# State products of an attention and MLP layer in four row groups and four PSUM banks, with the first transfers in another order

## The chip, the cores and the metric

The kernel runs on one core of a Trainium2 chip. Its engines work side by side, each through its own queue in order: TensorE (PE, with its weight loads PEld), VectorE (DVE), ScalarE (ACT), GpSimd (POOL) and SyncE (SP), which here issues the transfers. The metric is device time in microseconds (us). A page and a trace come from one execution that the hardware profiler recorded; its span runs from the first to the last instruction.

## The reference, cut to what matters

A layer for 8 sequences of 256 tokens of width 256: layer norm, then an attention with 16 heads and an MLP, both from the same normed input, added to the residual. All is float32. Per head, with 64 states:

```python
q, k = rope(hs @ Wq.T), rope(hs @ Wk.T)            # 128 a head
s = clip(hs @ Ws1.T @ Ws2.T + bs2, -32, 32)         # rank 16, then 64 states a head
z = cumlogsumexp(s, axis=tokens); es = exp(s); enz = exp(-z)
A = tril(q @ k.T * scale)
ok = enz * (A @ es)
W2 = tril((softmax(ok) * enz) @ es.T)
o = W2 @ v
o = o * rsqrt(mean(o * o) + eps) * g_norm_weight * silu(hs @ Wg.T)
out = o @ Wo.T
```

The MLP (2048 wide) has weights that come as 4-bit codes with scales, and are decoded on the chip.

## The kernel before

The 2048 tokens are taken in four groups of 512 (two sequences each), and the 16 heads in eight pairs: 32 steps of one group and one head pair, group after group. The main loop runs n from -1 to 32. In an iteration it prepares step n + 1 (`states` and the four `rope` calls, which make q and k), computes the scores of step n (`scores`, `logits`, `softmax`, and `value` and `gate`), and finishes step n - 1 (`turn`, `cross`, `weights`, `apply`, `outputs`, `turn_back`; every second time `close`, the output projection). Pieces of the MLP (`ffn`) and of the decoding (`decode_next`) are strewn between, so that TensorE has work while the attention's chain passes through the other engines.

The order is written by hand. Each piece has a place between 0 and 1 in the iteration: `POS` for all iterations, `START` for the first two, `NORM_AT` for the norm of a later token group, which `NORMS` puts into iterations 0, 2 and 5. `DUE` says how many decode pieces are to be issued by each iteration. The loop sorts the pieces by place and issues them. A piece issues its matmuls at once and leaves the work of the other engines as a generator in `chains`; after each piece `tick()` moves each generator on by one stage. So the places also decide how the queues of VectorE, ScalarE and GpSimd are ordered.

PSUM has eight banks of 512 float32 a partition. `bank()` gives one; where it is still read, the first matmul that writes it waits. The norm's scaled half and the rope's scratch share two buffers under one name, `z`.

`low_rank` (L374) makes the rank-16 product for a token group: two matmuls with `w_s1`, then one ScalarE copy with a bias, `one_at`, that sets row 16 of every group of 32 rows to one, so that the bias `bs2`, which lies as row 16 below `Ws2` in `w_s2`, is added by the second product. `rT` and `w_s2` hold two copies, at rows 0 and 32. `states` (L391) needs the second product both ways round: tokens by states (`es`, L402, from rows 0 to 16) and states by tokens (`esT`, L403, from rows 32 to 48). Each is four matmuls of 17 rows by 128 columns into one bank. VectorE clamps both (L413), ScalarE takes the exponential (L416), VectorE sums along the tokens (L421) and takes reciprocals (L427).

`rope` (L432): two matmuls (L438), two ScalarE copies that swap halves (L447, L448), one VectorE product with cos (L449), two GpSimd operations (L451, L452). `norm` (L185): VectorE statistics (L192 to L194), a GpSimd power (L195), the scaling into `z` (L198), transposes on TensorE (L206), a ScalarE copy to `xT` (L212). `softmax` begins with transposes (L548). `weights` multiplies (L618), and VectorE masks the two banks (L626).

Of the kernel before, what the change touches and what calls it, by code (L numbers as in the profile page):

```python
# [10 lines left out]
F32 = mybir.dt.float32  # L11
I32 = mybir.dt.int32
AF = mybir.ActivationFunctionType
ALU = mybir.AluOpType
# [18 lines left out]
POS = {'scores': (0.059, 0.112),  # L33
 'turn': (0,),
 'logits': (0.144,),
 'softmax': (0.255,),
 'cross': (0.143,),
 'weights': (0.179, 0.209),
 'low': (0.176,),
 'states': (0.223,),  # L40
 'outputs': (0.364, 0.394),
 'back': (0.647, 0.702),
 'close': (0.136, 0.286),
 'rope': (0.36, 0.45, 0.54, 0.63),
 'vg': (0.45, 0.55, 0.75, 0.88)}
START = {-1: {'states': (0.534,), 'rope': (0.3, 0.4, 0.5, 0.6)},
 0: {'vg': (0.0, 0.03, 0.06, 0.229),
     'scores': (0.2, 0.28),
     'states': (0.342,),
     'logits': (0.34,),  # L50
     'softmax': (0.5,),
     'rope': (0.16, 0.24, 0.32, 0.45)}}
FEED = {-1: (0.452, 1.0)}
NORMS = {0: 1, 2: 2, 5: 3}
NORM_AT = (0.2, 0.293, 0.427, 0.639, 0.75, 0.938)
FIRST = [0.35, 1.41]
LAST = [2.16, 2.05]
DUE = [4, 6, 6, 7, 8, 8, 10, 10, 11, 12, 12, 13, 14, 15, 15, 16, 17, 18, 18, 19, 20, 22, 23, 23, 24]


@with_exitstack
def layer_kernel(ctx: ExitStack, tc: tile.TileContext, a: dict, out: bass.AP):
# [74 lines left out]
    w_s1 = const.tile([P, 2, 64], F32, tag="w_s1", name="w_s1")  # L137
    w_s2 = const.tile([64, H * M], F32, tag="w_s2", name="w_s2")
    one_at = const.tile([64, 1], F32, tag="one_at", name="one_at")
# [17 lines left out]
    def load_w(n, k):  # L157

        if n < N:
            w = aw.tile([P, 2, 2, 2 * DK], F32, tag=f"wts{k}", name=f"wts{k}")  # L160
            nc.sync.dma_start(out=w, in_=a["wqkvg"][steps[n][1]][:, k : k + 2])
            wts[n, k] = w

    load_x(0, 2)
    load_x(2, 2)
    nc.sync.dma_start(out=w_s1.rearrange("p c f -> p (c f)"), in_=a["ws1"])
    nc.sync.dma_start(out=one_at, in_=a["one_at"])
    for r in (0, 32):
# [205 lines left out]
    def low_rank(g):  # L374

        need(*normed[g])
        rT = p1.tile([64, G], F32, tag="rT", name="rT")
        ps = bank()
        for c in range(2):
            nc.tensor.matmul(  # L380
                ps[0:64, :], lhsT=w_s1[:, c, :], rhs=xT[:, c, g * G : (g + 1) * G],
                start=c == 0, stop=c == 1,
            )

        def work():
            nc.scalar.activation(rT, ps[0:64, :], AF.Identity, bias=one_at)
            yield

        rTs[g] = rT, chain(work(), ps)

    def states(n):  # L391

        g, hp = steps[n]
        ms = slice(hp * P, (hp + 1) * P)
        (rT, c), to = rTs[g], of[n]
        need(c)
        es = to["es"] = new(p2, [P, TC, P], "es", 2)
        esT = to["esT"] = new(p2, [P, G], "esT", 2)
        ps, psT = bank(), bank()
        for i in range(TC):  # L400
            ts = slice(i * P, (i + 1) * P)
            nc.tensor.matmul(ps[:, ts], lhsT=rT[0:17, ts], rhs=w_s2[0:17, ms], start=True, stop=True)  # L402
            nc.tensor.matmul(  # L403
                psT[:, ts], lhsT=w_s2[32:49, ms], rhs=rT[32:49, ts], start=True, stop=True
            )


        enz = to["enz"] = new(p2, [P, G], "enz", 2)

        def work():  # L410
            both = ((esT, psT), (es.rearrange("p i m -> p (i m)"), ps))
            for t, q in both:
                nc.vector.tensor_scalar(t, q, CLAMP, -CLAMP, ALU.min, ALU.max)  # L413
            yield
            for t, q in both:
                nc.scalar.activation(t, t, AF.Exp)  # L416
            yield
            for b in range(2):
                e = esT[:, b * T : (b + 1) * T]

                nc.vector.tensor_tensor_scan(  # L421
                    enz[:, b * T : (b + 1) * T], e, e, 0.0, ALU.add, ALU.max
                )
            yield
            for i in range(TC):
                r = enz[:, i * P : (i + 1) * P]
                nc.vector.reciprocal(r, r)  # L427
                yield

        to["states"] = chain(work(), ps, psT, es, esT, enz)  # L430

    def rope(n, j, which):  # L432

# [373 lines left out]
def _layout(x):  # L807

    c = np.ascontiguousarray
    half = MLP // 2  # L810

    def pairs(ws):
        w = np.stack([w.T.reshape(P, 2, H // 2, 2 * DK) for w in ws])
        return c(w.transpose(3, 1, 0, 2, 4))

    def packed_in(w):
        return c(w.reshape(half, 2, -1).transpose(2, 1, 0).reshape(-1, MLP))

# [11 lines left out]
    return {  # L830
        "x": c(n[at + "hidden_states"].reshape(NTOK, D)),
        "wqkvg": pairs([n[at + w] for w in ("Wq", "Wk", "Wv", "Wg")]),
        "wo": c(n[at + "Wo"].T.reshape(H, DK, D).transpose(1, 0, 2)),
        "ws1": c(np.pad(n[at + "Ws1"].T.reshape(P, 2, 1, 16), [(0, 0)] * 3 + [(0, 16)]).repeat(2, 2).reshape(P, 128)),
        "one_at": (np.arange(64) % 32 == 16).astype(np.float32).reshape(64, 1),
        "ws2": c(n[at + "Ws2"].T),
        "bs2": c(n[at + "bs2"].reshape(1, H * M)),
        "gw": c(n[at + "g_norm_weight"].reshape(DK, 1)),
        "codes": quarters(lambda w: w, "_W_packed"),
        "scales": quarters(lambda w: w.repeat(16, 0), "_scales"),  # L840
        "cos": c(cos),
        "sin": c(sin),
    }
# [17 lines left out]
```

## Time and profile before

| | |
|---|---|
| time, median of 3 runs | 1268.24 us (1267.06 to 1269.0) |
| profiled execution, its own time | 1268.5 us |
| its span | 1266.5 us |
| busy DVE in the span | 795.7 us, 63% |
| first matmul | 7.08 us |
| end of the last matmul | 1262.3 us |
| all TensorE idle time up to the last matmul | 15.1 us |
| matmul records of L402 and L403 | 512, in 32 calls of 1.09 us |

The largest groups of TensorE are the products with the weights:

```profile
L438 PE MATMUL ps<-xT,wts 128*128 128x512 f32 x512 | 240.8, 593 | 0.0
L490 PE MATMUL ps<-wts,xT 128*128 128x256 f32 x1024 | 239.7, 379 | 0.0
```

A group line has the source line, engine and operation, what is written from what, the shapes and the count; then the busy time in us and the mean ns of one, then the idle time of the engine ahead of it. Matmuls overlap, so the mean of one is longer than the distance from one start to the next. A timeline line has start and length in us, engine, line and operation; in brackets is the engine's idle time ahead of it and what ended it. The list of waits has, for each pair, the us in all, the times and the longest.

### The profile page before, as it was taken

The numbers are of one execution on the slowest core, as the hardware profiler recorded it, in microseconds if no ns is written. First come the engines' busy times: TensorE is split into PE (matmuls) and PEld (weight loads), VectorE is DVE, ScalarE is ACT, GpSimd is POOL, SyncE is SP. The second block draws the span as 40 slices with busy tenths as digits, with TensorE's granted clock in tenths as the row PEclk, the third lists the DMA queues.
The fourth block names the chain that finished last, engine by engine and source line by source line (L and its number), as shares of the span: only waits on it lengthen the run. The fifth ranks groups of instructions, "written<-read, shape, count | busy, mean of one in ns | idle before, by whom it ended". The sixth has DMA issues, their size and how long they took to land.

```text
span 1266.5 us, 17998 instructions
## 1 busy us (share of the span) xinstructions
PE 1247.2 (98%) x6704; PEld 897.2 (71%) x6704; DVE 795.7 (63%) x1528; ACT 543.0 (43%) x1709; POOL 441.4 (35%) x408
## 2 busy tenths in 40 slices
PE   7999899999999999999999999999999999999998
PEld 4576676767777777767677686776777766777776
DVE  6967655766665666664765756666665566566443
ACT  2444335453444444452543534445443355445232
POOL 4444234441334443233443323444232444323311
PEclk9999999999999999999999999999999999999999
DMA  4301111011111100111110111101011110101000
GB/s 157 124 18 50 34 34 50 18 34 34 51 34 34 51 18 18 34 35 50 50 33 2 34 51 34 34 29 38 2 34 34 34 34 26 42 17 43 25 17 17
DMA packets 18362, 47.75 MB, mean 38 GB/s; under 512 B 1986, under 2 KB 6466, under 8 KB 18276
## 3 DMA queue, kind: packets, MB, share of 16 engines
q1 hardware_dynamic: 18276, 46.61, 11.5%
q8 instruction: 53, 0.87, 0.3%
q14 instruction: 33, 0.27, 0.1%
HBM read 44.51 MB, written 2.10 MB: 37 GB/s over the span
## 4 chain that ended last, share of the span: by engine, by line
PE 92%; DVE 5%; POOL 1%; issue 1%; ACT 1%; DMA 0%; POOLq 0%; DVEq 0%; ACTq 0%
PE ps L490 16%; PE ps L438 16%; PE ps L708 9%; PE ps L339 9%; PE ps L319 8%; PE ps L299 8%; PE ps L659 4%; PE ps L508 4%; PE ps L527 3%; PE ps L618 3%; PE ps L402 2%; PE ps L511 2%; PE ps L690 2%; PE ps L595 1%; PE ps L548 1%; PE ps L577 1%
## 5 line engine op out<-in xcount | busy, mean ns | idle before, releaser
L451 POOL TENSOR_TENSOR z<-z,sin 128x512 f32<-128x512 f32 x128 | 163.3, 1275 | 435.5 <-ACT z L448 434.8
L438 PE MATMUL ps<-xT,wts 128*128 128x512 f32 x512 | 240.8, 593 | 0.0
L490 PE MATMUL ps<-wts,xT 128*128 128x256 f32 x1024 | 239.7, 379 | 0.0
L490 PEld LDWEIGHTS ps<-wts,xT 128*128 128x128 f32 x1024 | 191.9, 190 | 55.8 <-issue 28.9
L438 PEld LDWEIGHTS ps<-xT,wts 128*128 128x128 f32 x512 | 94.3, 191 | 84.9 <-issue 77.8
L307 POOL TENSOR_SCALAR t<-t 128x512 f32<-128x512 f32 x64 | 40.2, 627 | 266.9 <-ACT t L305 256.5
L447 ACT COPY z<-ps 64x512 f32<-64x512 f32 x128 | 74.5, 582 | 129.8 <-PE ps L438 90.7
L299 PE MATMUL ps<-xT,w_gate 128*128 128x512 f32 x256 | 120.8, 594 | 0.0
L319 PE MATMUL ps<-xT,w_up 128*128 128x512 f32 x256 | 120.6, 593 | 0.0
L278 DVE TENSOR_TENSOR res<-ps,res 128x512 f32<-128x512 f32 x64 | 44.1, 689 | 117.0 <-PE ps L708 61.0
L427 DVE RECIPROCAL enz<-enz 128x128 f32<-128x128 f32 x128 | 116.7, 931 | 0.0
L339 PE MATMUL ps<-w_down,inter 128*128 128x256 f32 x512 | 116.0, 380 | 0.7 <-DVE inter L327 0.7
L708 PE MATMUL ps<-w_o,ogT 128*128 128x256 f32 x512 | 115.6, 379 | 0.0
L708 PEld LDWEIGHTS ps<-w_o,ogT 128*128 128x128 f32 x512 | 95.6, 190 | 14.6 <-issue 2.2
L339 PEld LDWEIGHTS ps<-w_down,inter 128*128 128x128 f32 x512 | 95.9, 190 | 14.2 <-DVE inter L327 1.5
L449 DVE TENSOR_TENSOR k<-ps,cos 128x512 f32<-128x512 f32 x64 | 43.9, 685 | 82.7 <-ACT z L448 82.7
L452 POOL TENSOR_TENSOR q<-q,z 128x512 f32<-128x512 f32 x64 | 81.6, 1274 | 21.6 <-DVE q L449 13.9
L452 POOL TENSOR_TENSOR k<-k,z 128x512 f32<-128x512 f32 x64 | 81.4, 1272 | 12.6 <-DVE k L449 8.3
L560 ACT ACTIVATE pr<-ps,mx 128x64 f32<-128x64 f32 x256 | 76.5, 325 | 12.8 <-DVE mx L557 12.8
L659 PEld LDWEIGHTS ps<-v,wt 128*128 128x128 f32 x512 | 65.0, 192 | 20.5 <-issue 19.8
L677 DVE SCALAR_TENSOR_TENSOR og<-ps,ss,sgate 128x128 f32<-128x128 f32 x256 | 70.0, 339 | 14.7 <-POOL ss L673 14.3
L673 POOL TENSOR_TENSOR ss<-ss,nhalf 128x4 f32<-128x4 f32 x64 | 64.8, 1017 | 39.8 <-DVE ss L672 38.1
(81 smaller groups left out, 1976.9 us busy)
## 6 DMA issues: line engine op xcount, KB each, us to landing
wts<-in_wqkvg_dram SPq DMA_DIRECT2D x64, 512.0 KB, 3.8
pk<-in_codes_dram SPq DMA_DIRECT2D x12, 256.0 KB, 4.7
sc<-in_scales_dram SPq DMA_DIRECT2D x12, 256.0 KB, 4.7
w_o<-in_wo_dram SPq DMA_DIRECT2D x4, 512.0 KB, 6.3
out_dram<-res SPq DMA_DIRECT2D x8, 256.0 KB, 2.1
res<-in_x_dram SPq DMA_DIRECT2D x3, 512.0 KB, 5.5
res<-in_x_dram SPq DMA_DIRECT2D x2, 256.0 KB, 3.4
w_s<-in_ws_dram SPq DMA_DIRECT2D x3, 64.0 KB, 2.8
```

The costliest lines, as they stand in the source:

```text
L299: nc.tensor.matmul(pg, lhsT=w_gate[:, c, ns], rhs=xT[:, c, gs], start=c == 0, stop=c == 1)
L319: nc.tensor.matmul(pu, lhsT=w_up[:, c, ns], rhs=xT[:, c, gs], start=c == 0, stop=c == 1)
L339: nc.tensor.matmul(ps[:, k, :], lhsT=inter[g, n][0][:, (i + k) * P : (i + k + 1) * P], rhs=w_dn[:, n, :], start=n == 2 * q, stop=n == 2 * ...
L427: nc.vector.reciprocal(r, r)
L438: nc.tensor.matmul(ps, lhsT=w[:, c, :], rhs=xT[:, c, g * G : (g + 1) * G], start=c == 0, stop=c == 1)
L447: nc.scalar.copy(z[0:64], pv[64:128])
L451: nc.gpsimd.tensor_tensor(z, z, sin_b, ALU.mult)
L452: nc.gpsimd.tensor_tensor(y, y, z, ALU.add)
L490: nc.tensor.matmul(ps[:, k, :], lhsT=xT[:, c, tt], rhs=w[:, which, c, :], start=c == 0, stop=c == 1,)
L560: nc.scalar.activation(pr[:, k, :], pv[:, k, :], AF.Exp, bias=mx[:, k : k + 1], scale=SCALE, accum_out=sm[:, k : k + 1],)
L659: nc.tensor.matmul(po[:, i, :], lhsT=wt[:, i, :], rhs=v[:, i, j * DK : (j + 1) * DK], start=False, stop=i == TC - 1,)
L708: nc.tensor.matmul(ps[:, k, :], lhsT=ogT[hh][0][:, (i + k) * P : (i + k + 1) * P], rhs=w_o[:, (hp // 2) * 4 + hh, :], start=hh == 0, stop= ...
```

## The change

`rT` and `w_s2` hold four copies, at rows 0, 32, 64 and 96 (`w_s1` and `one_at` grow to 128 columns and rows). `states` takes four banks instead of two: the tokens-by-states product comes from row groups 0 and 1, the other from 2 and 3, two matmuls for each group and bank. The clamp has four pieces of 256 columns, one for each bank. `Ws2` and `bs2` come from DRAM as one array of 17 rows.

At the start x (two halves, as before) and the first q and k weights lead SP's queue; `w_s1`, `one_at` and `cos` are issued from ScalarE's queue. The x of the second token group is loaded before the loop, ahead of the third code block. Places in `POS`, `START`, `NORM_AT` and two entries of `DUE` have new values. In the instruction order that follows from them, the first q product comes ahead of `low_rank`, `cross` behind `logits`, no decode pieces stand ahead of L626 in any step, and in iteration 2 the second half of the norm is scaled after the third rope, not after the fourth.

```diff
- 'softmax': (0.255,),
- 'cross': (0.143,),
- 'weights': (0.179, 0.209),
- 'low': (0.176,),
+ 'softmax': (0.232,),
+ 'cross': (0.179,),
+ 'weights': (0.179, 0.193),
+ 'low': (0.072,),
...
- 'back': (0.647, 0.702),
+ 'back': (0.647, 0.688),
...
- 'rope': (0.36, 0.45, 0.54, 0.63),
- 'vg': (0.45, 0.55, 0.75, 0.88)}
-START = {-1: {'states': (0.534,), 'rope': (0.3, 0.4, 0.5, 0.6)},
+ 'rope': (0.36, 0.45, 0.487, 0.63),
+ 'vg': (0.458, 0.566, 0.766, 0.838)}
+START = {-1: {'states': (0.544,), 'rope': (0.14, 0.43, 0.53, 0.63)},
...
-     'rope': (0.16, 0.24, 0.32, 0.45)}}
+     'rope': (0.198, 0.24, 0.32, 0.45)}}
...
-NORM_AT = (0.2, 0.293, 0.427, 0.639, 0.75, 0.938)
+NORM_AT = (0.2, 0.293, 0.427, 0.58, 0.75, 0.938)
...
-DUE = [4, 6, 6, 7, 8, 8, 10, 10, 11, 12, 12, 13, 14, 15, 15, 16, 17, 18, 18, 19, 20, 22, 23, 23, 24]
+DUE = [4, 6, 7, 7, 8, 8, 9, 10, 11, 12, 12, 13, 14, 15, 15, 16, 17, 18, 19, 19, 19, 22, 23, 23, 24]
...
     load_x(0, 2)
     load_x(2, 2)
-    nc.sync.dma_start(out=w_s1.rearrange("p c f -> p (c f)"), in_=a["ws1"])
-    nc.sync.dma_start(out=one_at, in_=a["one_at"])
-    for r in (0, 32):
-        nc.sync.dma_start(out=w_s2[r : r + 16, :], in_=a["ws2"])
-        nc.sync.dma_start(out=w_s2[r + 16 : r + 17, :], in_=a["bs2"])
+    nc.scalar.dma_start(out=w_s1.rearrange("p c f -> p (c f)"), in_=a["ws1"])
     load_w(0, 0)
-    nc.sync.dma_start(out=cos, in_=a["cos"])
+    nc.scalar.dma_start(out=one_at, in_=a["one_at"])
+    nc.scalar.dma_start(out=cos, in_=a["cos"])
     nc.sync.dma_start(out=sin, in_=a["sin"])
+    for r in range(0, P, 32):
+        nc.sync.dma_start(out=w_s2[r : r + 17, :], in_=a["ws2"])
...
-        ps, psT = bank(), bank()
-        for i in range(TC):
-            ts = slice(i * P, (i + 1) * P)
-            nc.tensor.matmul(ps[:, ts], lhsT=rT[0:17, ts], rhs=w_s2[0:17, ms], start=True, stop=True)
-            nc.tensor.matmul(
-                psT[:, ts], lhsT=w_s2[32:49, ms], rhs=rT[32:49, ts], start=True, stop=True
-            )
+        pss = [bank() for _ in range(4)]
+        for i in range(2):
+            for r, ps in enumerate(pss):
+                rows = slice(32 * r, 32 * r + 17)
+                k = 2 * (r % 2) + i
+                tok, st = rT[rows, k * P : (k + 1) * P], w_s2[rows, ms]
+                lhsT, rhs = (tok, st) if r < 2 else (st, tok)
+                nc.tensor.matmul(
+                    ps[:, i * P : (i + 1) * P], lhsT=lhsT, rhs=rhs, start=True, stop=True
+                )
...
-            both = ((esT, psT), (es.rearrange("p i m -> p (i m)"), ps))
-            for t, q in both:
-                nc.vector.tensor_scalar(t, q, CLAMP, -CLAMP, ALU.min, ALU.max)
+            both = (esT, es.rearrange("p i m -> p (i m)"))
+            for t, r in ((both[0], 2), (both[1], 0)):
+                for k in range(2):
+                    nc.vector.tensor_scalar(
+                        t[:, k * T : (k + 1) * T], pss[r + k][:, 0:T], CLAMP, -CLAMP,
+                        ALU.min, ALU.max,
+                    )
...
     load_w(0, 2)
+    load_x(TC, TC)
     load_packed(2)
...
-            put_at(0.0, load_x, gn * TC, TC)
+            if gn > 1:
+                put_at(0.0, load_x, gn * TC, TC)
```

More of the change, by code (lines that the diff above doesn't have):

```diff
@@ L135, in layer_kernel @@
     sin = const.tile([P, T], F32, tag="sin", name="sin")
-    w_s1 = const.tile([P, 2, 64], F32, tag="w_s1", name="w_s1")
-    w_s2 = const.tile([64, H * M], F32, tag="w_s2", name="w_s2")
-    one_at = const.tile([64, 1], F32, tag="one_at", name="one_at")
+    w_s1 = const.tile([P, 2, P], F32, tag="w_s1", name="w_s1")
+    w_s2 = const.tile([P, H * M], F32, tag="w_s2", name="w_s2")
+    one_at = const.tile([P, 1], F32, tag="one_at", name="one_at")
     gw = const.tile([P, 1], F32, tag="gw", name="gw")
@@ L376, in low_rank @@
         need(*normed[g])
-        rT = p1.tile([64, G], F32, tag="rT", name="rT")
+        rT = p1.tile([P, G], F32, tag="rT", name="rT")
         ps = bank()
@@ L380, in low_rank @@
             nc.tensor.matmul(
-                ps[0:64, :], lhsT=w_s1[:, c, :], rhs=xT[:, c, g * G : (g + 1) * G],
+                ps, lhsT=w_s1[:, c, :], rhs=xT[:, c, g * G : (g + 1) * G],
                 start=c == 0, stop=c == 1,
@@ L385, in work @@
         def work():
-            nc.scalar.activation(rT, ps[0:64, :], AF.Identity, bias=one_at)
+            nc.scalar.activation(rT, ps, AF.Identity, bias=one_at)
             yield
@@ L398, in states @@
         esT = to["esT"] = new(p2, [P, G], "esT", 2)
-        ps, psT = bank(), bank()
-        for i in range(TC):
-            ts = slice(i * P, (i + 1) * P)
-            nc.tensor.matmul(ps[:, ts], lhsT=rT[0:17, ts], rhs=w_s2[0:17, ms], start=True, stop=True)
-            nc.tensor.matmul(
-                psT[:, ts], lhsT=w_s2[32:49, ms], rhs=rT[32:49, ts], start=True, stop=True
-            )
+        pss = [bank() for _ in range(4)]
[8 more added lines that the diff above has]
+                )
         enz = to["enz"] = new(p2, [P, G], "enz", 2)
         def work():
-            both = ((esT, psT), (es.rearrange("p i m -> p (i m)"), ps))
-            for t, q in both:
-                nc.vector.tensor_scalar(t, q, CLAMP, -CLAMP, ALU.min, ALU.max)
+            both = (esT, es.rearrange("p i m -> p (i m)"))
[5 more added lines that the diff above has]
+                    )
             yield
-            for t, q in both:
+            for t in both:
                 nc.scalar.activation(t, t, AF.Exp)
@@ L428, in work @@
                 yield
-        to["states"] = chain(work(), ps, psT, es, esT, enz)
+        to["states"] = chain(work(), *pss, es, esT, enz)
     def rope(n, j, which):
@@ L833, in _layout @@
         "wo": c(n[at + "Wo"].T.reshape(H, DK, D).transpose(1, 0, 2)),
[L834 to L837, printed above, removed]
+        "ws1": c(np.pad(n[at + "Ws1"].T.reshape(P, 2, 1, 16), [(0, 0)] * 3 + [(0, 16)]).repeat(4, 2).reshape(P, 256)),
+        "one_at": (np.arange(P) % 32 == 16).astype(np.float32).reshape(P, 1),
+        "ws2": c(np.concatenate([n[at + "Ws2"].T, n[at + "bs2"].reshape(1, H * M)])),
         "gw": c(n[at + "g_norm_weight"].reshape(DK, 1)),
```

## The prediction

> **What bounds the kernel now.** I read the page's busy shares first, then the chain that ended last, then who made TensorE wait, then the stretches of the span, and at last the timeline around the one operation whose form changes.
>
> ```profile
> PE 1247.2 (98%) x6704; PEld 897.2 (71%) x6704; DVE 795.7 (63%) x1528; ACT 543.0 (43%) x1709; POOL 441.4 (35%) x408
> ...
> PE 92%; DVE 5%; POOL 1%; issue 1%; ACT 1%; DMA 0%; POOLq 0%; DVEq 0%; ACTq 0%
> ```
>
> TensorE is busy for 98% of the span and holds 92% of the chain; the next engine has more than a third of its time free. A microsecond less of TensorE work should be a microsecond less of time, wherever TensorE doesn't wait. So where does it wait?
>
> ```profile
> PE ps L206 <- DVE z L198: 12.3, 4, 7.1
> PE ps L527 <- DVE at L498: 1.5, 1, 1.5
> PE ps L380 <- ACT xT L212: 0.7, 1, 0.7
> PE ps L339 <- DVE inter L327: 0.7, 2, 0.5
> ...
> 20.00:42.00 22.00, 22.00 (x85) 14.15 (x83) 21.86 (x34) 10.00 (x18) 11.94 (x10) 1.00 0.31 96
> 42.00:66.00 24.00, 20.43 (x98) 12.20 (x97) 22.99 (x47) 9.22 (x28) 10.54 (x11) 1.00 0.37 132
> 66.00:1240.00 1174.00, 1170.40 (x6401) 849.46 (x6400) 733.48 (x1409) 513.28 (x1639) 409.72 (x368) 1.00 0.10 33
> ```
>
> The columns of the last three lines are stretch, length, then busy time of PE, PEld, DVE, ACT, POOL. From 66 to 1240 us TensorE loses 3.6 us in 1174. From 20 to 66 it is VectorE that is full (44.85 of 46 us), and TensorE loses 3.6 us there. Ahead of that lie 7.1 us before the first transpose. So there are three regimes: a start that waits for data, some 46 us that VectorE sets, and 1174 us that TensorE sets.
>
> The operation that changes, in the step at 262 us:
>
> ```profile
> 261.50 0.61 PE L644 MATMUL ps<-cross,prT 64*128 64x128 f32 x8
> 261.82 1.28 DVE L626 TENSOR_TENSOR wt<-ps,mask 128x512 f32<-128x512 f32 x2
> 262.04 0.37 PE L402 MATMUL ps<-w_s,rT 17*128 17x128 f32 x1
> 262.05 0.37 PE L403 MATMUL ps<-rT,w_s 17*128 17x128 f32 x1
> 262.25 0.27 PE L402 MATMUL ps<-w_s,rT 17*128 17x128 f32 x1
> 262.26 0.27 PE L403 MATMUL ps<-rT,w_s 17*128 17x128 f32 x1
> 262.36 0.27 PE L402 MATMUL ps<-w_s,rT 17*128 17x128 f32 x1
> ...
> 262.93 0.27 PE L403 MATMUL ps<-rT,w_s 17*128 17x128 f32 x1
> 263.13 0.65 PE L548 MATMUL ps<-ident,ok 128*128 128x128 f32 x4
> 263.25 0.69 DVE L413 TENSOR_SCALAR esT<-ps 128x512 f32<-128x512 f32 x1
> ```
>
> A float32 matmul leaves two records, so the eight matmuls are sixteen. They start in pairs, L402 in rows 0 to 16 and L403 in rows 32 to 48, 0.01 us apart; pairs follow at 0.11 us, after a first gap of 0.21 and before a last of 0.20. One call costs 263.13 - 262.04 = 1.09 us, the same in all 32 calls: 34.9 us.
>
> **What the Trainium skill says.** "TensorE: Matmul & The Clock Gate", section Part 3 (Packing small matmuls), says that matmuls in different row groups run side by side, and gives 3.07 times for four groups of K=32, N=512. The trace agrees for two groups: a pair takes 0.11 us, what one 128-column record of L659 takes with all 128 rows (1.05 us for eight). No run yet shows four. "TensorEngine Tiling (Array Packing)", section Restrictions and Gotchas, says that row tiles can't write one PSUM bank at once; L402 and L403 do write two. Four groups thus need four banks, half of the eight. "DMA: Bandwidth & Descriptors", section Issuing engines are not separate DMA queues, says that a second issuing queue saves only the issuing time and shares the same transfer engines. The trace of before has one queue only, so it can't say.
>
> **The change part by part.** Sums are against the profiled execution: 1268.5 us, span 1266.5, and so 2 us around it; the median of the runs is 1268.24, 0.26 lower.
>
> *States in four groups.* Each group does two matmuls, four records, instead of eight. With full overlap the starts are 0, 0.21, 0.32, 0.43 and the next work comes 0.21 later: 0.65 us, 0.44 less. That is the best case, since one group can't go faster than a record in 0.11. By the page's 3.07 of 4, records would come at 0.11 x 4 / 3.07 = 0.143, and the call takes 0.75. If the array takes only one pair at a time, nothing is saved. I take 0.44, as the trace shows two groups without loss. 30 calls lie in the TensorE-bound stretch: **-13.2**; the first two are counted with the start.
>
> *Its cost on VectorE.* Four clamps of 256 columns replace two of 512. 512 columns take 0.60 us from start to start, 128 columns (L677) 0.26, so 256 about 0.37: 1.48 against 1.20, some 0.28 us a step. After 66 us VectorE has 440 us free; there it costs nothing. In the VectorE-bound start two calls cost 0.6.
>
> *Its cost in banks.* From first write to last read, four banks are live when states starts in 29 of 32 steps: the two output banks and the two of L618 that L626 is reading. With four more, all eight are taken. In the changed order the transposes after states reuse the first L626 bank, and the work after them the second. In the step shown these are free at about 262.50 and 263.10. TensorE would come at 262.04 + 0.65 = 262.69 and 263.18: margins of 0.19 and 0.08. In the step at 222.72 four decode operations stood ahead of L626, which ended at 224.77 and 225.37 only; that would have cost 1.4 us. In the changed VectorE order no step has decode work there; at most one operation of 0.6 us (L308 or L312) stands between the product and the masks. I put **+1.0** for all steps (0.03 each), as the second margin is almost nothing.
>
> *The start.* The first q-k product now goes ahead of the low-rank product. In before, L380 at TensorE's slow initial pace (four records in 3.6 us) took 10.0 to 13.6, and VectorE stood idle from 12.4 until ScalarE had copied the first product:
>
> ```profile
> 10.00 3.68 PE L380 MATMUL ps<-xT,w_s 128*64 128x512 f32 x4 [0.68 <-ACT xT L212]
> 13.61 4.86 PE L438 MATMUL ps<-xT,wts 128*128 128x512 f32 x10
> ...
> 17.14 0.69 DVE L449 TENSOR_TENSOR q<-ps,cos 128x512 f32<-128x512 f32 x1 [4.72 <-ACT z L448]
> ```
>
> Now that product takes the slow slot, 10.0 to 13.5, so L449 can start at about 15 instead of 17.1. The head weights must be there by 10.0: with them, x and the low-rank weights 1.18 MB are ahead, and at the rates of before (143 GB/s to 5 us, 245 after) they land at 6.9. VectorE gains 2.1, pays 0.6 for clamps, and its work from there to 66 us is otherwise the same. So the end of the full stretch comes about 1.5 us earlier, with a further 0.5 because the second norm half's z is put ahead of a reciprocal and L327 (1.55 us), which shortens the 1.63 us wait at 58 us: **-2.0**. TensorE's own saving of 0.88 in the first two calls is inside this, not on top: VectorE sets the pace there. Low-rank weights on ScalarE's queue start beside x; in the worst case x lands 131 KB later, 0.4 us at 334 GB/s. The table load waits behind three issues of about 0.5 each, but ScalarE's first copy is at 8.4. The four loads of 17 rows are needed at 19, the last issue is near 4. They cost nothing. SP issues three fewer ahead of the codes, and the bytes ahead of them grow by 0.2 MB, 0.6 us: about even, with VectorE idle until 15 anyway. If that cover went, the first decode group would be late by the same 0.6. The early load of the second x group (0.5 MB, used at 41.6) goes ahead of the third code block and is also covered.
>
> *The wait at 130 us.* This is the one loss in the steady part.
>
> ```profile
> 130.81 1.26 POOL L452 TENSOR_TENSOR k<-k,z 128x512 f32<-128x512 f32 x1
> ...
> 132.11 1.91 DVE L198 TENSOR_SCALAR z<-res,mv,rstd 128x256 f32<-128x256 f32 x2 [2.07 <-POOL k L452]
> 133.46 0.36 PE L206 MATMUL ps<-ident,z 128*128 128x128 f32 x1 [3.35 <-DVE z L198]
> ```
>
> The normalised half waits for a z buffer that the fourth q-k product's GpSimd work frees. With the new positions that z is written after the third product; the fourth has the other buffer. GpSimd's third add ended at 128.11 in before, and in the new order L307 comes after it, 0.7 us earlier still. So z starts at about 127.4 and the transposes at 128.7, where TensorE arrives at about 130.1 minus three calls, 128.8, minus the start's gain. Some 0.4 us may be left of 3.6: **-3.2**.
>
> *Only moved.* The cross product goes behind the logits product: same records, and its ScalarE copy still has the 1.5 us of L618 and L644 before its bank is wanted. Decode pieces, gates and turn-backs shift by a block or two under free VectorE time: nothing.
>
> Sum: -13.2 + 1.0 - 2.0 - 3.2 = -17.4, so 1251.1 against the profiled time, or **1250.8** against the median.
>
> **The rivals.** *Only the steady states gain.* The start stays bound by VectorE and the 130 us wait moves rather than goes (GpSimd's backlog speaks for it; the freed buffer against): 1268.2 - 13.2 + 1.0 = 1256.0.
>
> *Four groups go no faster than two.* The sequencer, not the array, spaces the pairs: for it, no place in the trace has denser starts; against it, two records start 0.01 us apart, far closer than the 0.027 that four in 0.11 need. Then -2.0 + 0.9 - 3.2 + 1.0: 1264.9.
>
> *Slower: bank waits at L548's place.* All eight banks are taken, the transposes wait for L626, and states itself for the last readers. Each us per step is 32 us. It decides from 18.4 / 32 = 0.57 us a step; at 1 us the time is 1268.2 - 18.4 + 32 = 1281.8. For it speak the margins of 0.08 and 0.19 us, against it the cleared VectorE order.
>
> **How the numbers follow.** Forecast 0.69, only the steady states 0.16, no gain from four groups 0.09, bank waits 0.06. The forecast's own range is 1246.5 to 1255 (the page's 3.07 alone adds 3; a larger start gain takes 3 away). To hold 8 in 10 it must take in the second case: 1246 to 1258.5. A difference under 0.2% (2.5 us) can't be told from none. Faster 0.91 (the third case is 3.3 us faster, near the edge: part of it counts as same), same 0.03, slower 0.06.
>
> **What would show it.** Right: states' records in fours at 0.11 us, 0.65 us a call; no PE wait over 0.2 us after 66 us, none for L206 at 130; the first L449 near 15 us. Wrong: records still in pairs; or PE waits on L626's readings or the clamps in every step, which would sink it.

## The result, and the profile after

| | before | after |
|---|---|---|
| time, median of 6 runs | 1268.61 us (1267.06 to 1269.38) | 1256.93 us (1256.84 to 1258.36) |
| ratio to before, 95% interval | | 0.9913 [0.9901, 0.9926] |
| profiled execution, its own time | 1268.5 us | 1258.18 us |
| its span | 1266.5 us | 1256.2 us |
| a call of the states' products, steady | 1.09 us | 0.66 us |
| first VectorE product of a rope | 17.14 us | 21.94 us |
| third call of the states' products | 71.39 us | 76.22 us |
| the wait at 130 us | 3.35 + 0.26 us | 2.16 us |

The change gains 11.7 us; 17.4 were forecast. The table says where the rest is: 30 steady calls gain 30 x 0.43 = 12.9 us, more than the whole, and the start gives 4.8 us back. One run of an experiment below (rows16_sp) took 1624 us at a mean clock of 0.748 and is left out of its figures. In the code after, the lines that matter are L406 (states' matmuls), L416 (clamps), L444 and L455 (the rope's matmuls and its VectorE product), L632 (masks), L554 (the transposes behind states), L197 and L205 (the norm's scaling and transposes), L298, L308 and L312 (the MLP's gate product and two VectorE operations on it), L250 (first decode operation), L172, L227 and L228 (loads of `w_s2`, codes and scales).

The page's first and fourth part, after: busy us of each engine, and the shares of the chain that ended last.

```profile
PE 1236.6 (98%) x6704; PEld 889.1 (71%) x6704; DVE 798.8 (64%) x1592; ACT 541.9 (43%) x1709; POOL 441.3 (35%) x408
...
PE 92%; DVE 5%; DMA 1%; issue 1%; POOL 1%; ACT 0%; POOLq 0%; ACTq 0%; SPq 0%; DVEq 0%
```

TensorE still sets the end. The small new entry is DMA: 1% of the chain, where before it was 0%. The list of what TensorE waited for, after:

```profile
PE ps L205 <- DVE z L197: 7.9, 2, 7.3
PE ps L298 <- DVE t L312: 2.2, 1, 2.2
PE ps L298 <- DVE q L455: 2.1, 1, 2.1
PE ps L533 <- DVE at L504: 1.6, 1, 1.6
...
PE ps L406 <- DMA w_s<-in_ws_dram: 0.4, 1, 0.4
```

Nothing here is a wait on the masks (L632) or on the clamps (L416): the two extra banks cost nothing that shows. New are the 2.1 us for a rope's first product, the 0.4 us for `w_s2` itself and, in a line left out here, 0.5 us in two waits of the transposes L583. The same stretches as before, after the change (length, busy PE, PEld, DVE, ACT, POOL, the granted clock, DMA share and GB/s):

```profile
20.00:42.00 22.00, 19.87 (x72) 12.53 (x73) 21.45 (x34) 7.79 (x14) 11.98 (x10) 0.92 0.22 66
42.00:66.00 24.00, 21.22 (x90) 11.26 (x89) 22.60 (x50) 10.67 (x31) 11.89 (x12) 0.97 0.42 145
66.00:1232.00 1166.00, 1163.84 (x6432) 845.03 (x6431) 742.20 (x1477) 514.07 (x1645) 410.98 (x371) 1.00 0.11 33
```

The last stretch is as it was: full, with 2.2 us lost, all at one place. VectorE is full from 20 to 66 us as before, only it has more left to do at 20. And the clock column, which was 1.00 before, shows 0.92 and 0.97. The operation that was changed, in the step at 262 us (timeline of TensorE after):

```profile
261.93 0.38 PE L406 MATMUL ps<-w_s,rT 17*128 17x128 f32 x2
261.94 0.38 PE L406 MATMUL ps<-rT,w_s 17*128 17x128 f32 x2
262.14 0.28 PE L406 MATMUL ps<-w_s,rT 17*128 17x128 f32 x2
262.16 0.28 PE L406 MATMUL ps<-rT,w_s 17*128 17x128 f32 x2
...
262.59 0.65 PE L554 MATMUL ps<-ident,ok 128*128 128x128 f32 x4
```

Each line holds two records, so four start within 0.01 us, the next four 0.2 us later, and the last two fours, at 262.26 and 262.37, 0.1 us apart. The call takes 262.59 - 261.93 = 0.66 us.

Then the start (timelines of VectorE and TensorE after):

```profile
20.34 0.49 DVE L250 TENSOR_SCALAR u<-pk 128x256 int32<-128x256 int32 x2 [11.79 <-DMA pk<-in_codes_dram]
...
21.94 0.68 DVE L455 TENSOR_TENSOR q<-ps,cos 128x512 f32<-128x512 f32 x1
...
22.68 2.67 PE L298 MATMUL ps<-xT,w_gate 128*128 128x512 f32 x4 [2.13 <-DVE q L455]
```

VectorE stands still for 11.79 us, and what ends it is the first block of the MLP's codes. Before, the same wait was 2.37 us and ended at 10.73. The rope's first product could have started at about 15, since ScalarE's copy for it ended at 15.06, but it stands behind the decode operation in VectorE's queue. So the first product of the start's full stretch comes 4.8 us later than before instead of 2 us earlier, and the rest of the stretch with it. The code transfers were issued at 5.6 to 8.5 us. Why did they take until 20? SyncE's timeline after shows its issues (start, length of issue):

```profile
2.68 2.89 SPq L172 DMA_DIRECT2D w_s<-in_ws_dram  x4
5.62 0.36 SPq L227 DMA_DIRECT2D pk<-in_codes_dram  x1
7.17 0.35 SPq L228 DMA_DIRECT2D sc<-in_scales_dram  x1
7.56 0.43 SPq L227 DMA_DIRECT2D pk<-in_codes_dram  x1
8.03 0.43 SPq L228 DMA_DIRECT2D sc<-in_scales_dram  x1
10.72 0.33 SPq L161 DMA_DIRECT2D wts<-in_wqkvg_dram  x1
13.45 0.38 SPq L152 DMA_DIRECT2D res<-in_x_dram  x1
16.49 0.33 SPq L227 DMA_DIRECT2D pk<-in_codes_dram  x1
19.75 0.33 SPq L228 DMA_DIRECT2D sc<-in_scales_dram  x1
```

The last four issues, 2.7 to 3.3 us apart, start as the four `w_s2` loads complete: each was held until one of them had landed, at 10.71, 13.44, 16.47 and 19.74 us. So each load of 17 rows, 68 KB, takes some 3 us, one after the other: 68 / 3 = 23 GB/s. In slices of 0.75 us, the DMA rate from 22.5 to 25.5 us, where nothing but shares left behind these loads can still be under way, is 20 to 26 GB/s; the highest rate of before in such slices is 426 GB/s, and 426 / 16 = 27. The loads of 17 rows run at the rate of one transfer engine in sixteen.

The semaphore updates in the traces show what this does to the codes. The first block, issued at 5.62 us, gives sixteen updates: fifteen come between 7.93 and 8.35 us, and the last, which VectorE waits for, at 20.31, 0.6 us after the last load of 17 rows. Before, all sixteen came between 9.43 and 10.71. So fifteen sixteenths of the block had landed 12 us before the rest.

The Trainium skill has the reason, in "DMA: Bandwidth & Descriptors", section Why a DMA increments its semaphore by 16 and not by 1: a transfer is spread over the largest number of engines, up to 16, that divides the slowest dimension of both its sides, and 127 partitions are among its examples for one engine. By that rule 16 rows go to 16 engines and 17 rows to one. It also says that the semaphore jumps at once for the engines that take no part; the trace of after agrees: each of these loads has one update soon after its issue (at 3.15 us for the first) and one at its end (10.71), where a load of 16 rows has sixteen spread over its end (rows16, below: 6.90 to 9.64 us for the first).

The second loss is the wait at 130 us (timelines of VectorE and TensorE after):

```profile
130.52 2.02 DVE L197 TENSOR_SCALAR z<-res,mv,rstd 128x256 f32<-128x256 f32 x2 [2.08 <-POOL q L458]
132.46 0.67 DVE L308 TENSOR_TENSOR t<-ps,t 128x512 f32<-128x512 f32 x1
133.83 0.69 DVE L312 SCALAR_TENSOR_TENSOR t<-t,ps 128x512 f32<-128x512 f32 x1 [0.69 <-ACT t L310]
...
134.57 1.98 PE L298 MATMUL ps<-xT,w_gate 128*128 128x512 f32 x4 [2.16 <-DVE t L312]
```

The scaled half does follow the third rope now (`q`, before it was the fourth, `k`), and the transposes no longer wait. But L308 and L312 stand behind the scaling in VectorE's queue, and L312 is the last reader of the bank that the gate product L298 writes next. So the wait moved there, at 2.16 us.

### The profile page after: what moved, and what is told of

It is laid out like the page before. It is cut to its first block, busy times and chain, and to the rows that moved or that the text cites. A ratio compares the mean times of both kernels' runs of the same rounds, so it can differ in the third digit from the quotient of the medians.

```text
span 1256.2 us, 18066 instructions
## 1 busy us (share of the span) xinstructions
PE 1236.6 (98%) x6704; PEld 889.1 (71%) x6704; DVE 798.8 (64%) x1592; ACT 541.9 (43%) x1709; POOL 441.3 (35%) x408
## 4 chain that ended last, share of the span: by engine, by line
PE 92%; DVE 5%; DMA 1%; issue 1%; POOL 1%; ACT 0%; POOLq 0%; ACTq 0%; SPq 0%; DVEq 0%
PE ps L496 16%; PE ps L444 16%; PE ps L714 9%; PE ps L338 9%; PE ps L298 8%; PE ps L318 8%; PE ps L514 4%; PE ps L665 4%; PE ps L533 4%; PE ps L624 3%; PE ps L517 2%; PE ps L696 2%; PE ps L406 2%; PE ps L554 1%; DMA pk<-in_codes_dram 1%; PE ps L601 1%
## 5 line engine op out<-in xcount | busy, mean ns | idle before, releaser
L444 PE MATMUL ps<-xT,wts 128*128 128x512 f32 x512 | 243.5, 599 | 0.7 <-ACT xT L211 0.7
L496 PE MATMUL ps<-wts,xT 128*128 128x256 f32 x1024 | 236.6, 379 | 0.0
L444 PEld LDWEIGHTS ps<-xT,wts 128*128 128x128 f32 x512 | 95.2, 193 | 80.4 <-issue 72.6
L298 PE MATMUL ps<-xT,w_gate 128*128 128x512 f32 x256 | 121.5, 597 | 4.3 <-DVE t L312 2.2
L458 POOL TENSOR_TENSOR q<-q,z 128x512 f32<-128x512 f32 x64 | 81.5, 1273 | 27.9 <-DVE q L455 23.8
L455 DVE TENSOR_TENSOR k<-ps,cos 128x512 f32<-128x512 f32 x64 | 43.8, 684 | 63.2 <-ACT z L454 63.2
L310 ACT ACTIVATE t<-t 128x512 f32<-128x512 f32 x64 | 40.3, 630 | 97.8 <-DVE t L308 97.8
L609 ACT COPY cross<-ps 128x256 f32<-128x256 f32 x32 | 11.9, 372 | 161.3 <-PE ps L601 160.8
```

Source lines behind the costliest of these rows:

```text
L298: nc.tensor.matmul(pg, lhsT=w_gate[:, c, ns], rhs=xT[:, c, gs], start=c == 0, stop=c == 1)
L444: nc.tensor.matmul(ps, lhsT=w[:, c, :], rhs=xT[:, c, g * G : (g + 1) * G], start=c == 0, stop=c == 1)
L458: nc.gpsimd.tensor_tensor(y, y, z, ALU.add)
L496: nc.tensor.matmul(ps[:, k, :], lhsT=xT[:, c, tt], rhs=w[:, which, c, :], start=c == 0, stop=c == 1,)
```

## The experiments

Each ran beside the kernel before on the same chip. "rows16" is the kernel after with one repair; several others are edits of it. The first question was the start: the four loads on one transfer engine, or the second queue and the new order of the transfers?

**rows16**: each load of 17 rows as one of 16 rows and one of a single row.

```diff
-        nc.sync.dma_start(out=w_s2[r : r + 17, :], in_=a["ws2"])
+        nc.sync.dma_start(out=w_s2[r : r + 16, :], in_=a["ws2"][0:16, :])
+        nc.sync.dma_start(out=w_s2[r + 16 : r + 17, :], in_=a["ws2"][16:17, :])
```

> The changed kernel with each of the four loads of 17 rows split into one of 16 rows and one of a single row; nothing else. Theory T (one engine): each 17-row load runs on a single transfer engine, 3 us of its time each, so four of them keep one engine of sixteen busy until 19.7 us, and the sixteenth part of each code block that this engine carries lands at 20 to 22 us. Split, the rows spread over sixteen engines: the first code block is complete near 10.5 us, the first decode starts near 11, the first L449 product near 15 instead of 21.9, the TensorE wait of 2.1 us at 20.6 and the half-clock stretch at 23.8 are gone, the second states call starts near 46 instead of 51.6, and the time is about 1251 (6 less). Rival R (the second queue and 0.2 MB more ahead of the codes): the number of engines of a load doesn't matter; the codes stay late and the time stays at 1257.

Measured: 1251.81 us (1250.92 to 1253.2), ratio to before 0.9872 [0.9857, 0.9886], against 0.9913 [0.9901, 0.9926] for the kernel after; the intervals don't meet. That is 5.1 us less, with four more transfers. Run once more beside other kernels (rows16_again), it took 1251.48 us (1250.69 to 1253.08), 0.9873 [0.9858, 0.9889].

> rows16 once more, on the same chip as the other two: 1251 to 1252.5 if the repair of the four loads holds, with no half-clock stretch in the trace; over 1255 if the first measurement was luck.

VectorE's timeline in rows16 (a line later than after: the rope's product is L456):

```profile
12.81 0.49 DVE L251 TENSOR_SCALAR u<-pk 128x256 int32<-128x256 int32 x2 [4.34 <-DMA pk<-in_codes_dram]
...
15.10 0.69 DVE L456 TENSOR_TENSOR q<-ps,cos 128x512 f32<-128x512 f32 x1 [0.39 <-ACT z L455]
```

The decode comes 7.5 us earlier than after, and the rope's first product waits for ScalarE's copy at 15.10, where the prediction had put it. The sixteen updates of the first code block come together, between 12.28 and 12.78 us. That is nearly 2 us later than I expected: SyncE issued the block only at 10.25 us (5.62 in after), since it waited 3.5 us for `cos` to land before it issued the third of the four single rows. The third call of states comes at 69.89 instead of 76.22. TensorE's waits and the same stretches in rows16:

```profile
PE ps L339 <- DVE inter L327: 1.3, 2, 1.1
PE ps L299 <- DVE t L313: 1.3, 1, 1.3
```

```profile
20.00:42.00 22.00, 22.00 (x78) 14.01 (x77) 21.47 (x39) 9.21 (x17) 11.69 (x12) 1.00 0.24 79
42.00:66.00 24.00, 21.41 (x102) 12.75 (x101) 22.47 (x45) 9.26 (x28) 9.89 (x9) 1.00 0.39 132
66.00:1232.00 1166.00, 1164.71 (x6429) 843.04 (x6427) 741.45 (x1481) 517.81 (x1655) 413.27 (x372) 1.00 0.10 33
```

The 2.1 us wait for L455 and the 0.4 us for `w_s2` are gone, the 20 to 42 us stretch is full again, and the clock is 1.00 in all three.

**half17**: the same repair for two of the four loads only, those of rows 0 and 32. A rival that depends on the queue or the order, not on the loads, gives all or nothing here.

```diff
+        if r < 64:
+            nc.sync.dma_start(out=w_s2[r : r + 16, :], in_=a["ws2"][0:16, :])
+            nc.sync.dma_start(out=w_s2[r + 16 : r + 17, :], in_=a["ws2"][16:17, :])
+        else:
+            nc.sync.dma_start(out=w_s2[r : r + 17, :], in_=a["ws2"])
```

> The changed kernel with two of the four 17-row loads (rows 0 and 32) split into 16 and 1 rows, and two left whole: the dose. Theory T (3 us of one engine for each whole load, in a row): the two whole loads are through near 13.5 us instead of 19.7, the first code block and its scales near 14 to 15, the first decode starts at 14 to 15 and L449 follows at about 16.2, one us later than with none whole; the waits of TensorE at 20 us and the half-clock stretch don't appear. Time 1252 to 1253.5, near rows16 (1251.8) and far from the changed kernel (1256.9). If the loss grew evenly with the whole loads, it would be 1254.4.

Measured: 1253.3 us (1253.27 to 1253.38), 0.9881 [0.9865, 0.9898]. VectorE's first decode operation in half17:

```profile
15.55 1.40 DVE L254 TENSOR_SCALAR u<-pk 128x256 int32<-128x256 int32 x2 [6.93 <-DMA pk<-in_codes_dram]
```

12.81, 15.55 and 20.34 us for none, two and four such loads. The effect follows their number, but not evenly in time: the first two cost 1.5 us of the whole (this against rows16's 1251.81), the other two 3.6, perhaps since VectorE waits for ScalarE's copy until 15.10 in any case, and covers part of the first delay. The rope's product came at 18.05, later than expected, since the decode operations that arrive late stand ahead of it.

**sp_queue**: after, with ScalarE's three loads back on SyncE's queue and the loads of 17 rows kept. **rows16_sp**: the same edit in rows16.

```diff
-    nc.scalar.dma_start(out=w_s1.rearrange("p c f -> p (c f)"), in_=a["ws1"])
+    nc.sync.dma_start(out=w_s1.rearrange("p c f -> p (c f)"), in_=a["ws1"])
...
-    nc.scalar.dma_start(out=one_at, in_=a["one_at"])
-    nc.scalar.dma_start(out=cos, in_=a["cos"])
+    nc.sync.dma_start(out=one_at, in_=a["one_at"])
+    nc.sync.dma_start(out=cos, in_=a["cos"])
```

> The changed kernel with the low-rank weights, one_at and cos issued on SP's queue at the same places in the program, the 17-row loads kept. Theory T: the codes still wait behind four 17-row loads on one engine; three more issues ahead make it no better: 1256.5 to 1258.5, the first decode still at 20 us or later. x lands 0.2 us earlier, as the low-rank weights no longer start beside it, so the first transpose is back at 7.1. Rival R: without the second queue the codes land near 11 as before, and the time falls to about 1251.

> rows16 with the low-rank weights, one_at and cos issued on SP's queue: what ScalarE's queue brings once no load sits on one engine. Three issues of 0.5 us move ahead of the head weights and the codes; the weights still land before 10 us, the codes 1.4 us later, before L449 needs VectorE; x lands 0.2 to 0.4 us earlier. Expected 1251 to 1252.5, no difference. If the second queue carries the start, it is 2 us slower, as with the whole loads (1259.3 against 1256.9).

Measured: sp_queue 1259.31 us (1257.82 to 1260.15), 0.9929 [0.9914, 0.9943], with the first decode at 21.32; rows16_sp 1251.34 us (1250.33 to 1251.6, three runs), 0.9864 [0.9847, 0.988], as rows16. The second queue is not the cause: without it the decode is no earlier, and with the loads repaired it makes no difference that these runs can tell. It may cost x something: in the five traces with one queue the first transposes start at 6.46 to 7.08 us, in the seven with two at 7.14 to 7.35, but the difference is covered.

**two_groups**: rows16 with the states' products as they were before, in two row groups and two banks, with two clamps.

```diff
-        pss = [bank() for _ in range(4)]
-        for i in range(2):
-            for r, ps in enumerate(pss):
...
+        ps, psT = bank(), bank()
+        for i in range(TC):
+            ts = slice(i * P, (i + 1) * P)
...
```

> rows16 with the states products back in two row groups and two banks and clamps of 512 columns; order and places as in the changed kernel. Theory T, in which four groups save 0.43 us of TensorE time in each of the 30 calls that TensorE bounds: 12.9 us more than rows16, about 1264. Rival (the gain comes from the new order and the start, and the four groups give back in bank waits and clamps what they save): within 4 us of rows16.

Measured: 1263.71 us (1262.63 to 1264.63), 0.9961 [0.9947, 0.9975]; its calls take 1.09 us again. Four groups are worth 11.9 us, of which 30 x 0.43 = 12.9 us were to come from the steady calls.

**states_only**: the kernel before, with four row groups, banks, copies and clamps alone: old order, old places, loads of 16 rows and one row.

```diff
-    for r in (0, 32):
+    for r in range(0, P, 32):
...
-        ps, psT = bank(), bank()
+        pss = [bank() for _ in range(4)]
...
```

> The kernel before with only the states products in four groups and four banks (four copies of the weights, loaded as 16 and 1 rows as before, on SP's queue); all places and the rest of the start as before. Theory T with bank waits in the old order: 13 us saved by the calls; given back are about 1.5 us where decode work stands ahead of the L626 masks (two steps), and about 1 us at the start since the head weights are issued 1.3 us later: 1257 to 1259. If the new order is needed for the four banks (the bank-wait rival of the prediction), PE waits on L626 or the clamps show in most steps and the time stays above 1263. If the new places brought nothing but the start, states_only lies as far above rows16 as the start differs, 4 to 8 us.

Measured: 1261.04 us (1260.18 to 1262.87), 0.9945 [0.9931, 0.996]: a gain of 7.0 us at the medians where the calls alone give 12.9. Two of the calls' followers are late; the step at 222 us in states_only, TensorE and VectorE:

```profile
222.15 0.38 PE L406 MATMUL ps<-w_s,rT 17*128 17x128 f32 x2
...
224.26 0.66 PE L554 MATMUL ps<-ident,ok 128*128 128x128 f32 x4 [1.39 <-DVE wt L632]
...
221.93 0.49 DVE L251 TENSOR_SCALAR u<-pk 128x256 int32<-128x256 int32 x2
...
222.91 0.69 DVE L256 SCALAR_TENSOR_TENSOR w_gate<-u,sc 128x512 f32<-128x512 f32 x1
223.52 1.28 DVE L632 TENSOR_TENSOR wt<-ps,mask 128x512 f32<-128x512 f32 x2
```

Decode operations stand ahead of the masks, the masks are the readers of the bank that L554 takes, and TensorE waits 1.39 us, in two steps (222 and 781 us): 2.8 us. The wait at 130 us is still there too, 3.79 us long, with a stretch of half clock behind it from 134.2 to 137.6. So the moved places of the change, with the changed entries of `DUE` (they are four, not two), are no ornament: they take away the masks' waits, and the wait at 130 us in part. My expectation missed by 2 us. 2.8 of the 5.9 us missing against the calls are the masks' waits; the rest, longer waits in the start among it (those at 44 and 58 us are 1.84 and 2.01 us for 1.46 and 1.63), is not accounted for line by line.

**before_norm**: the kernel before with two places moved, so that in iteration 2 the norm's second half is scaled after the third rope, and nothing else.

```diff
- 'rope': (0.36, 0.45, 0.54, 0.63),
+ 'rope': (0.36, 0.45, 0.487, 0.63),
...
-NORM_AT = (0.2, 0.293, 0.427, 0.639, 0.75, 0.938)
+NORM_AT = (0.2, 0.293, 0.427, 0.58, 0.75, 0.938)
```

> The kernel before with two places moved, and nothing else: the third rope from 0.54 to 0.487 and the second half of the norm from 0.639 to 0.58. In iteration 2 the half is then scaled after the third rope. If the wait of 3.35 us at 130 us shrinks to 0.4 to 2 us and takes the half-clock stretch that follows it (3.4 us long, so about 1.7 us of TensorE time) with it, the gain is 1.4 to 3.2 us of wait plus 1.7 us of clock: about 1264.2 against 1268.4. If the stretch after it has nothing to do with the wait and stays, about 1265.9. If the wait only moves to another instruction, 1268.

Measured: 1265.61 us (1265.0 to 1267.6, 21 runs), 0.9981 [0.9975, 0.9988]. The 21 runs fall in two groups by the granted clock: sixteen at a mean clock of 1.0 took 1265.0 to 1265.95 us, five at 0.998 took 1267.21 to 1267.6. The profiled one is of the second kind. Its TensorE and VectorE timelines, and the stretches there:

```profile
128.17 1.13 DVE L198 TENSOR_SCALAR z<-res,mv,rstd 128x256 f32<-128x256 f32 x2 [2.08 <-POOL q L452]
129.23 0.68 DVE L309 TENSOR_TENSOR t<-ps,t 128x512 f32<-128x512 f32 x1
130.60 0.69 DVE L313 SCALAR_TENSOR_TENSOR t<-t,ps 128x512 f32<-128x512 f32 x1 [0.70 <-ACT t L311]
...
131.34 3.58 PE L299 MATMUL ps<-xT,w_gate 128*128 128x512 f32 x4 [2.38 <-DVE t L313]
```

```profile
130.00:131.40 1.40, 0.06 (x1) 0.06 (x1) 0.69 (x1) 1.36 (x3) 0.21 (x1) 0.92 0.78 246
131.40:134.00 2.60, 2.60 (x3) 1.12 (x4) 1.89 (x3) 2.58 (x6) 2.08 (x2) 0.50 0.75 259
134.00:138.00 4.00, 4.00 (x24) 3.29 (x23) 2.46 (x6) 2.05 (x4) 2.19 (x3) 0.93 0.02 5
```

A wait of 2.38 us is left, with the same instruction as in the kernel after, and then TensorE runs at half clock (0.50) for a while: the four records of L299 take 3.58 us, after the change 1.98. The two moves gain 2.9 us at the medians, but the wait itself shrinks by 1.2 us only. The rest is in the main the stretch of half clock (3.4 us long in the kernel before, 133.7 to 137.1, so up to 1.7 us of work). All 25 executions of the kernel before that ran beside it have a mean clock below 1.0 (0.995 or 0.999), of these 21 only five; there the stretch costs 2.0 us (1267.4 against 1265.5, the middles of the two groups). The sum is rough, since the moves act in other iterations too: the third call of states starts at 71.96 us, 0.6 later than before.

**rows16_wo** and **rows16_h0** ask what holds the rest of that wait. The first puts GpSimd's scaling of `w_o`, which stands between its rope operations, at the head of iteration 2. The second transposes the first norm half at 0.58, before the second is scaled at 0.6, in iteration 2 alone.

```diff
-                put_at(0.3 + 0.04 * h, scale_wo, h)
+                put_at(0.01 * h, scale_wo, h)
```

```diff
-            put_norm(gn, NORM_AT)
+            put_norm(gn, NORM_AT if n != 2 else (0.2, 0.293, 0.427, 0.6, 0.58, 0.938))
```

> rows16 with the four GpSimd scalings of w_o (1.12 us each) at the head of iteration 2, where GpSimd is idle from 99 to 105 us, instead of between the ropes. Theory: the wait left at 126 us (1.29, L299 behind L313 behind the scaled norm half behind GpSimd's third rope add) comes from GpSimd's queue, in which two scalings stand ahead of that add; 2.2 us of it go, the wait goes, and the time falls by 1.3 to about 1250.5. If the norm's half is late for another reason (the ropes' own order), the wait stays.

> rows16 with one more move, in iteration 2 alone: the first norm half is transposed at 0.58, before the second is scaled, which comes at 0.6. If what is left of the wait there (1.29 us in rows16) comes from the second half standing in VectorE's queue ahead of the work that TensorE needs next, it falls to about 0.8 us: 0.3 to 0.8 us faster than rows16. If it comes from GpSimd's third addition, which ends at about 124.2, it stays or only changes its place: no change against rows16.

Measured: rows16_wo 1251.41 us (1250.91 to 1251.97), 0.9866 [0.9852, 0.9881], as rows16; GpSimd's third addition ends at 123.95 us against 124.16. The theory of a `w_o` backlog falls: without the scalings GpSimd waits 1.35 us instead of 0.25 for the third rope's copies, which wait for the shared buffer. The wait of TensorE is 1.61 us, but another one: the moved pieces shift other operations too (L313 now stands behind the fourth rope's product), and ScalarE's copy L701 ends it. rows16_h0: 1249.95 us (1249.67 to 1251.12), 0.9859 [0.9845, 0.9872]. VectorE and the steady stretch in rows16_h0:

```profile
124.90 0.69 DVE L309 TENSOR_TENSOR t<-ps,t 128x512 f32<-128x512 f32 x1 [2.78 <-POOL t L307]
125.51 1.03 DVE L198 TENSOR_SCALAR z<-res,mv,rstd 128x256 f32<-128x256 f32 x2
```

```profile
66.00:1232.00 1166.00, 1165.62 (x6432) 844.80 (x6431) 741.48 (x1481) 517.18 (x1655) 412.54 (x372) 1.00 0.10 33
```

L309 now stands ahead of the scaling, and TensorE loses 0.4 us in 1166. The wait of 1.3 us is gone altogether, more than I expected; the theory that VectorE's queue order holds it stands. The time is 1.5 us below rows16_again at the medians, and three of its four runs are below all eight of rows16 and rows16_again, but the ratios' intervals overlap: a likely gain, not an established one. It is the fastest kernel of this study. A third buffer for the norm's half, which would part it from the ropes, was not tried.

## Why the prediction was right or wrong

The measured time is on the forecast's side and inside the wide range (1246 to 1258.5), but 6 us above the forecast and outside its own range, which ends at 1255. It lies within 1 us of the first rival's 1256.0, for which the range had been widened, but not by that rival's account: there the start stayed as it was, while here it got 4.8 us worse. That the wide range held is in part luck.

| step | forecast | measured, and in what |
|---|---|---|
| states in four groups | -13.2 | 30 x (0.66 - 1.09) = -12.9 in the trace; 11.9 by two_groups |
| bank waits | +1.0 | no such wait in after; +2.8 in the old order (states_only) |
| the start | -2.0 | +4.8 in after, -1.5 in rows16 (third call of states) |
| the wait at 130 us | -3.2 | -1.45 of wait, -1.7 of clock; -2.9 alone (before_norm) |

The measured terms give -12.9 + 4.8 - 3.15 = -11.2, against 1258.18 - 1268.5 = -10.3 of the profiled executions; 0.9 us is not accounted for.

*Four groups.* Right, in form and size: fours at 0.1 us, 0.66 us a call for 0.65. The page's 3.07 of 4, given for N=512 (0.75 us a call here), is not what this case shows; the array took the four groups without loss. The four clamps take 1.33 us in the step at 262 us (262.79 to 264.12), where 1.48 was worked out.

*Bank waits.* Right in mechanism, and none came where 1.0 us was allowed for; the rival that ends slower is ruled out by the waits' list of after. The 1.4 us that the prediction worked out for the step at 222.72, were decode operations ahead of the masks, is the 1.39 us of states_only. In the new order no wait on the masks shows in any step.

*The start: here the prediction failed.* The step is the one that priced the transfers: "The four loads of 17 rows are needed at 19, the last issue is near 4. They cost nothing", and behind it "about even" for the codes. It counted bytes and issues at rates of the whole DMA (143 to 334 GB/s), as if every transfer were spread over 16 engines. Four loads of 17 rows instead of two of 16 and two of 1 put 272 KB on one engine, and each later transfer has a share that stands behind them there. The loads themselves came too late as well: the last landed at 19.74 us, and the states' products waited 0.4 us for it. A cover was named, "VectorE idle until 15 anyway", and the price if it went, 0.6 us; the codes came at 20.3, where they had come at 10.7. In rows16, where only this is repaired, the step comes out as forecast: L456 at 15.10 for "about 15", the start 1.5 us earlier for 2.0. That the loads are the cause is shown (rows16, half17). That they run on one engine follows from their rate, their end times and the page, and from the one late update in sixteen of the codes behind them; the traces don't name the engine of a transfer.

*The wait at 130 us.* The size is right by two errors that cancel, which is luck. The wait did not fall to 0.4 us. The third addition was to end at 127.4, with L307 behind it. In before_norm it ended at 128.13, in the span as late as before (128.11); but there all of this step comes 0.6 us later, so that most of the 0.7 us for L307's place was gained, and a wait of 0.24 us for ScalarE's copy (L448) took the rest. What failed is the queue: L308 and L312 stand behind the scaling on VectorE, with TensorE's next bank behind them. The prediction asked who frees the `z` buffer, and not what is queued behind the instruction that waits for it. rows16_h0 shows it: with L309 ahead of the scaling the wait is gone. Against it, the price of the wait was more than its length: the half-clock stretch behind it, which the prediction didn't count, went too.

With the start repaired, the forecast of 1250.8 is met within about 1 us by rows16 (1251.81 and 1251.48), though its terms differ both ways: the wait left there is 1.29 us for 0.4, and the half-clock stretch is gone.

## What to carry to other kernels

Before merging two loads into one, look at the row count: here 16 + 1 rows in two transfers were better than 17 in one, by 5.1 us. The harm fell less on the loads themselves (a wait of 0.4 us) than on what was issued after them, where it shows as a wait on another tensor.

When a wait is taken from an instruction, go through the queue behind it on the same engine up to the next reader of a bank that TensorE wants, since the wait can land there, as 2.16 us of it did here. And a TensorE wait can cost more than its length: after some waits here the clock was halved for 3.4 us, so look at the clock column beside the waits.

## What the runs showed of the hardware that was not expected

- One transfer of 17 rows, 68 KB, took about 3 us (10.71, 13.44, 16.47, 19.74 us at its four ends), and codes issued at 5.62 us landed at 20.31. With 16 rows and one row in its place the codes were there at 12.8, though issued 4.6 us later.
- The half-clock stretch is 3.4 us long in each of these: 133.7 to 137.1 before, 23.8 to 27.2 and 64.8 to 68.2 after; in sp_queue it is twice as long, 51.8 to 58.6. Count windows of 3.413 us from the first full clock (14.26 us before, 13.60 after). In the clock records of all twelve traces every later change of the clock falls on an edge of these windows: the 35th and 36th before, the 3rd, 4th, 15th and 16th after.
- The length of a wait alone doesn't decide: 2.38 us (before_norm) was followed by a stretch, 2.16 us at 132 us in after was not. What divides most cases is how long TensorE stood idle, by its matmul records, within the window just ahead. A stretch followed 3.15 us (before), 2.99 (states_only), 2.19 (before_norm), 2.12 (after, the first) and 1.84 (sp_queue). Windows of up to 1.62 us had none behind them, and the wait of 2.16 us lies across an edge, with 0.64 and 1.51 us on its two sides. Two half-clock windows don't fit: after's second follows 1.07 us of idle time, and the second of sp_queue's pair follows none to speak of. So this is a pattern of these traces and not the whole rule.
- "TensorE: Matmul & The Clock Gate", section What's actually happening, says that the hardware watches a free-running window of about 3.4 us and that the effect therefore varies from run to run. The runs agree with the length, with the fixed edges and with the variation (five of 21 executions of before_norm); the idle times above are all shorter than that window.
- The six runs of after took 1256.84 to 1256.96 us (four, mean clocks 0.999 to 1.0) and 1258.18 and 1258.36 us (0.997 and 0.999). A mean clock of 0.999 stands beside 1256.84 and 1258.36 alike, so what a stretch costs there, where VectorE sets the pace, is left open.
